# Three mixtures of experts of a decoder: blocks of tokens sorted by expert in all three, fetched by indirect reads

## The chip, the cores and the metric

The kernel runs on one core of a Trainium2 chip. One launch computes a whole decoder of four layers. The metric is the device time of that launch in microseconds (us). Three timed runs of the kernel before took 1896.66, 1902.3 and 1903.81 us; their median, 1902.3 us, is the time before. A further execution was recorded by the hardware profiler, and every figure of a view below comes from that one.

The engines of the core are named as in the profile: PE (matmuls) with its weight loads PEld, DVE and ACT (elementwise work, reductions, activations), POOL (elementwise work and the issue of indirect DMAs) and SP (which issues the plain DMAs here). Each takes its instructions in order; semaphores order them among each other.

## The reference

The input x has 4 x 256 = 1024 tokens of 128 numbers. Every layer adds a self attention, a cross attention and a feed-forward part to x, each on a normalised copy. Layer 0, 1 and 2 have a mixture of experts as feed-forward part; layer 3 has a plain one. Only the mixtures matter here (x stands for the normalised tokens):

```python
# layer 0: 32 experts, one for each token, inner width 256, and a shared expert
ids = argmax(x @ gate_w); s = sigmoid(max(x @ gate_w))
routed = (silu((x*s) @ g[ids]) * ((x*s) @ u[ids])) @ d[ids]
out = shared_swiglu(x) + routed
# layer 1: 8 experts, the best two for each token, inner width 512
w = softmax(top2(x @ gate_w.T))
out = sum_k w[k] * (silu(x @ w1[e_k].T) * (x @ w3[e_k].T)) @ w2[e_k].T
# layer 2: 8 experts, the best two for each token, inner width 512, with biases
p = softmax(x @ gate_w.T)
out = sum_k p[e_k] * (relu(x @ w1[e_k] + b1[e_k]) @ w2[e_k] + b2[e_k])
```

A mixture may be computed densely (each expert on all tokens, with weight nought for most) or sparsely (each expert only on its own tokens).

## The kernel before

x stays in SBUF for the whole launch as eight tiles of 128 tokens. The launch is a row of stages, each with its own pools of SBUF and PSUM: `layer_0` (both attentions), `ffn0`, `layer_1`, `strided_attention`, `ffn1`, `linear_attention`, `latent_attention`, `ffn2`, `layer_3`, `quantised_ffn`. The last lines of `decoder` call them in this order. The scheduler of the language puts the instructions of each engine in an order of its own and adds the semaphores; where a pool takes over the memory of one that is closed, its first users wait for the users of the old one.

**`ffn0` (line 895) is sparse.** `all_normalised_T` (793) gives the normalised tokens and their transposes, `logits_of` (799) the gate's logits, `top` (810) one-hot choices. `blocks_of` (830) sorts: it counts each expert's tokens (851), ranks each token within its expert (842 to 848) with triangular and all-one matrices, gives each expert as many blocks of 128 slots as it needs, and ends with `index` (a slot for each token) and `at` (for each block the columns of its expert in the weights). There are 1024/128 + 31 = 39 blocks at most, 4992 slots. A DRAM tensor `sent` is filled with zeros (908); then eight indirect DMAs on POOL store the tokens into their slots (920). Groups of four blocks are read back by plain DMAs (960) and transposed (966). For each block, `hidden` (970) multiplies by the gate and up matrices of its expert, whose columns the PE finds with a register loaded from `at` (890); SiLU and product follow; `turned` (982) transposes, `result` (989) multiplies by the down matrix, and each group is stored to `done` in DRAM (1003). The three work on blocks b, b-1 and b-2 in one turn. At the end eight indirect DMAs read each token's row from `done` (1020), and DVE adds it (1024). The shared expert (926 to 951) is computed between the stores and the blocks. The weights e0h (8 MB) and e0d (4 MB) lie in SBUF.

**`ffn1` (1043) and `ffn2` (1080) are dense.** Expert by expert, its weights come in one slab (1062, 1116). All 1024 tokens are multiplied (1069, 1120), put through the activation (1076 and 1077; 1127 and 1129), multiplied by the second matrix, and added to x with the weight of this expert for each token (`add_weighted`, 1026, with the matmuls of 1033 and the additions of 1039). In `ffn2` the second bias is one product of the weights with b2 (1107) and the first comes with the activation.

Between `ffn0` and `layer_1` SP loads the weights of all later attentions into the pool `late` (1692), 2 MB of them for `latent_attention` (w2x).

A matmul in f32 leaves two records in the trace.

Of the kernel before, what the change touches and what calls it, by code (L numbers as in the profile page):

```python
# [83 lines left out]
def _constants():  # L84
# [11 lines left out]
    iota = np.tile(np.arange(32), (P, 1))  # L96
# [11 lines left out]
) = np.cumsum([0, 128, 128, 72, 4, 32, 4, 4, 4, 1, 128, 64]).tolist()  # L108


def _layout(i):
# [53 lines left out]
    a["gates"] = _cat(  # L165
        f["L0_ffn_gate_w"], f["L1_ffn_gate_w"].T, f["L2_ffn_gate_w"].T,
        f["L2_ffn_b1"].reshape(8, 4, P).transpose(2, 0, 1).reshape(P, 32),
    )
    a["b2"] = f["L2_ffn_b2"]
# [8 lines left out]
    def down(w):  # L178
        return w.reshape(8, 4, P, P).transpose(0, 2, 1, 3).reshape(8, P, 512)

    a["e1"] = np.ascontiguousarray(np.concatenate([
        f["L1_ffn_w1"].transpose(0, 2, 1), f["L1_ffn_w3"].transpose(0, 2, 1),
        down(f["L1_ffn_w2"].transpose(0, 2, 1)),
    ], 2))
    a["e2"] = np.ascontiguousarray(np.concatenate([f["L2_ffn_w1"], down(f["L2_ffn_w2"])], 2))
# [7 lines left out]
def decoder(ctx: ExitStack, tc: tile.TileContext, dr, out):  # L193
# [636 lines left out]
    def blocks_of(pool, hots, size, widths):  # L830
# [7 lines left out]
        for i, h in enumerate(hots):  # L838
            V.tensor_copy(hb[:, i * NT : (i + 1) * NT, :], h)

# [8 lines left out]
        count = ps("t")[:n_e, :P]  # L849
        for i in range(n):  # L850
            T.matmul(count, lhsT=hb[:, i, :], rhs=onesb, start=i == 0, stop=i == n - 1)
# [12 lines left out]
        full = small.tile([P, 32], F32, tag="full", name="full")[:, :n_e]  # L864
        V.tensor_scalar(full, cum[:, 32 : 32 + n_e], partition, None, ALU.is_le)

        ex = small.tile([P, 3], F32, tag="ex", name="ex")
        V.tensor_reduce(ex[:, 2:3], full, AX.X, ALU.add)
        for i, wd in enumerate(widths):
            V.tensor_scalar(ex[:, i : i + 1], ex[:, 2:3], n_e - 1.0, float(wd), ALU.min, ALU.mult)  # L870
        xp = ps("t")
        for i in range(2):
            T.transpose(xp[:1, i * P : (i + 1) * P], ex[:, i : i + 1], ident)
        at = pool.tile([1, 2, P], I32, tag="at", name="at", bufs=1)
        V.tensor_copy(at, xp[:1, :S].rearrange("p (i b) -> p i b", i=2))
# [10 lines left out]
        return index, at  # L886

    def offset(at, i, b, most):

        return nc.values_load(  # L890
            at[0:1, i, b : b + 1], engines=[mybir.EngineType.PE], min_val=0, max_val=most,
            skip_runtime_bounds_check_because="the number of an expert, limited to the last one's",
        )

    def ffn0(wh):


        size = 39
        with ExitStack() as st:
            st.enter_context(psum_pool("psf0"))  # L900
            pool = st.enter_context(tc.tile_pool(name="ffn0", bufs=2))
            dram = st.enter_context(tc.tile_pool(name="ffn0d", bufs=1, space=bass.MemoryType.DRAM))
            wd = load("e0d", pool=pool)
            sent = dram.tile([size * P, D], F32, tag="sent", name="sent")
            done = dram.tile([size * P, D], F32, tag="done", name="done")
            nought = pool.tile([P, D], F32, tag="nought", name="nought", bufs=1)
            G.memset(nought, 0.0)
            nc.sync.dma_start(
                sent.rearrange("(n p) d -> p n d", p=P),
                nought.unsqueeze(1).to_broadcast([P, size, D]),  # L910
            )
            xn = [pool.tile([P, D], F32, tag=f"xn{t}", name=f"xn{t}", bufs=1) for t in range(NT)]
            xnT = all_normalised_T(pool, keep=xn, tag="t")
# [3 lines left out]
            index, at = blocks_of(pool, [hot], size, (512, 256))  # L917
            for t in range(NT):
                V.tensor_scalar(xn[t], xn[t], score[:, t : t + 1], None, ALU.mult)
                G.indirect_dma_start(  # L920
                    out=sent[:, :], out_offset=bass.IndirectOffsetOnAxis(ap=index[:, t : t + 1], axis=0),
                    in_=xn[t], in_offset=None,
                )


            for c in range(2):
# [24 lines left out]
                )  # L951


            groups = [range(b, min(b + 4, size)) for b in range(0, size, 4)]
            xbT, h, hT, y = {}, {}, {}, {}

            def fetch(g):
                n = len(groups[g])
                xb = pool.tile([P, 4, D], F32, tag="xb", name="xb", bufs=3)
                nc.sync.dma_start(  # L960
                    xb[:, :n, :],
                    sent[4 * g * P : (4 * g + n) * P, :].rearrange("(n p) d -> p n d", p=P),
                )
                tp = ps("t")
                for i in range(n):
                    T.transpose(tp[:, i * P : (i + 1) * P], xb[:, i, :], ident)
                xbT[g] = pool.tile([P, 512], F32, tag="xbT", name="xbT")
                A.copy(xbT[g][:, : n * P], tp[:, : n * P])

            def hidden(b):  # L970
                o = ps("g")
                at_h = offset(at, 0, b, 31 * 512)
                T.matmul(
                    o, lhsT=xbT[b // 4][:, b % 4 * P : (b % 4 + 1) * P],
                    rhs=wh[:, bass.ds(at_h, 512)], start=True, stop=True,
                )
                sg = pool.tile([P, 256], F32, tag="sg", name="sg", bufs=3)
                A.activation(sg, o[:, :256], AF.Silu)
                h[b] = pool.tile([P, 256], F32, tag="h", name="h", bufs=3)
                V.tensor_tensor(h[b], sg, o[:, 256:], ALU.mult)  # L980

            def turned(b):
                tp = ps("t")
                for i in range(2):
                    T.transpose(tp[:, i * P : (i + 1) * P], h[b][:, i * P : (i + 1) * P], ident)
                hT[b] = pool.tile([P, 256], F32, tag="hT", name="hT", bufs=3)
                V.tensor_copy(hT[b], tp[:, :256])

            def result(b):
                g, i = b // 4, b % 4  # L990
                if i == 0:
                    y[g] = ps("y")
                at_d = offset(at, 1, b, 31 * 256)
                for ic in range(2):
                    T.matmul(
                        y[g][:, i * P : (i + 1) * P], lhsT=hT[b][:, ic * P : (ic + 1) * P],
                        rhs=wd[:, bass.ds(at_d + ic * P, P)], start=ic == 0, stop=ic == 1,
                    )
                if b == groups[g][-1]:
                    n = len(groups[g])  # L1000
                    ys = pool.tile([P, 4, D], F32, tag="ys", name="ys")
                    A.copy(ys[:, :n, :], y[g][:, : n * P].rearrange("p (n d) -> p n d", n=n))
# [6 lines left out]
            for b in range(size + 2):  # L1009
                if b % 4 == 1 and b // 4 + 1 < len(groups):  # L1010
                    fetch(b // 4 + 1)
                if b < size:
                    hidden(b)
# [707 lines left out]
```

## Time and profile before

| | us |
|---|---|
| median of three timed runs | 1902.3 |
| profiled execution | 1916.55 |
| its span, first to last instruction | 1914.7 |
| ffn0: last addition of layer 0's attention to the first matmul of layer 1 | 321.0 to 463.1 |
| ffn1: last addition of the strided attention to the first matmul of the linear attention | 619.3 to 799.4 |
| ffn2: last addition of the latent attention to the first matmul of layer 3 | 1406.3 to 1537.1 |

How to read the views. The page gives busy time, share of the span and count of instructions of each engine, and then groups: line, engine, operation, what is written and read, shapes, count, busy time in us, mean time of one in ns, and after the second bar the idle time of the engine just before, with what ended most of it. The timeline gives start, duration, engine, line, operation and count of runs of equal instructions, and in brackets the idle time before. The list of DMA issues gives tile, queue, count, KB of each and median us from issue to landing. PEq, PEldq, SPq and so on are an engine's sequencer. The profiled execution is 14 us longer than the median of the others; differences within it are read as shares of it.

### The profile page before, as it was taken

To read this page: it belongs to the slowest core of one execution; us is meant where nothing else is said; L and a number is where in the kernel's file an instruction comes from. 1 tells how busy PE (TensorE), PEld (TensorE's weight loads), DVE (VectorE), ACT (ScalarE), POOL (GpSimd) and SP (SyncE) were. 2 spreads that over 40 slices of the span, in tenths; PEclk is the share of its full clock that TensorE was granted. 3 is DMA by queue.
4 is the path that set the end of the run, shared out by engine and by line. 5 is a ranking of instruction groups with operands and counts; after the bars stand their busy time and mean duration, and the time that the engine had idled before them with its cause. 6 is when DMAs were issued, how large, how long until landed. Compare 5 with 4: busy or idle time off the path is not lost. (4 is left out here: it accounts for less than half of the span.)

```text
span 1914.7 us, 27552 instructions
## 1 busy us (share of the span) xinstructions
PE 1651.3 (86%) x10756; PEld 887.9 (46%) x10756; DVE 884.3 (46%) x2886; ACT 709.2 (37%) x1307; POOL 239.1 (12%) x391
## 2 busy tenths in 40 slices
PE   6999997694977999755889999999999989999873
PEld 3443333362456566544344554545567744433332
DVE  4565552242744333544743434434233355655526
ACT  1444445131621212100466566566621114344441
POOL 5221000105120000221200000000000041211000
PEclk9999997796966899855989999999999959999985
DMA  7000002323000110000000000000011000000000
GB/s 262 1 1 1 1 1 101 90 60 105 2 1 14 53 49 17 1 0 6 1 1 1 1 1 1 1 1 1 1 45 34 12 26 1 1 1 1 1 1 11
DMA packets 26193, 43.69 MB, mean 23 GB/s; under 512 B 2504, under 2 KB 20176, under 8 KB 24784
## 3 DMA queue, kind: packets, MB, share of 16 engines
q1 hardware_dynamic: 25552, 40.89, 6.1%
q8 instruction: 85, 1.39, 0.3%
q0 software_dynamic: 512, 1.05, 0.2%
q14 instruction: 44, 0.36, 0.1%
HBM read 35.77 MB, written 6.16 MB: 22 GB/s over the span
## 5 line engine op out<-in xcount | busy, mean ns | idle before, releaser
L492 PE MATMUL s<-kc,qm 32*128 32x256 f32 (+1 forms) x1024 | 239.0, 579 | 10.4 <-POOL qm L449 4.2
L554 PE MATMUL s<-qm,kc 32*128 32x512 f32 (+1 forms) x896 | 230.5, 629 | 1.4 <-POOL qm L449 1.4
L571 ACT ACTIVATE pr<-s 128x512 f32<-128x512 f32 x256 | 137.9, 596 | 187.8 <-PE s L554 184.9
L499 DVE TENSOR_REDUCE mx<-s 128x1 f32<-128x512 f32 (+1 forms) x192 | 123.2, 686 | 110.4 <-PE s L554 98.9
L1431 ACT ACTIVATE ss<-ss,ntop 128x768 f32<-128x768 f32 x128 | 118.6, 928 | 100.6 <-DVE ntop L1429 100.3
L285 POOL TENSOR_SCALAR ve<-mv 128x2 f32<-128x2 f32 (+1 forms) x64 | 14.2, 223 | 1124.9 <-DVE mv L283 1120.4
L590 PE MATMUL o<-pr,v 128*32 128x256 f32 (+1 forms) x1792 | 146.6, 395 | 4.1 <-ACT os L596 3.7
L492 PEld LDWEIGHTS s<-kc,qm 32*128 32x128 f32 x1024 | 98.1, 211 | 76.9 <-DVE mx L503 26.2
L1033 PEld LDWEIGHTS pt<-slab,hT 128*128 128x128 f32 x1024 | 118.5, 192 | 11.3 <-issue 8.8
L1425 DVE CUSTOM_DVE_ANT_0 ss<-f,n 128x512 f32<-128x512 f32 x128 | 83.7, 688 | 80.3 <-PE f L1420 80.3
L1033 PE MATMUL pt<-slab,hT 128*128 128x128 f32 x1024 | 119.3, 276 | 0.0
L503 DVE CUSTOM_DVE_ANT_0 junk<-s,nmif 128x512 bf16<-128x512 f32 x128 | 83.3, 689 | 70.8 <-PE s L492 70.7
L1069 PE MATMUL sc<-xnT,slab 128*128 128x512 f32 x256 | 115.4, 605 | 0.0
L1491 PE MATMUL o<-pr,v 128*64 128x256 f32 x768 | 113.6, 402 | 0.0
L573 ACT ACTIVATE pr<-s,n 128x512 f32<-128x512 f32 x128 | 80.3, 685 | 73.9 <-PE s L554 73.6
L1471 PE MATMUL s<-qT,kT 64*128 64x256 f32 x768 | 107.5, 394 | 0.0
L449 POOL TENSOR_SCALAR qm<-q,consts 128x256 f32<-128x256 f32 x80 | 73.1, 930 | 207.3 <-ACT q L446 147.8
L590 PEld LDWEIGHTS o<-pr,v 128*32 128x32 f32 x1792 | 40.3, 110 | 122.3 <-issue 99.6
L1478 ACT ACTIVATE pr<-s,n 128x512 f32<-128x512 f32 x128 | 80.6, 679 | 27.8 <-PE s L1471 27.6
L548 PE MATMUL s<-mT,selg 12*128 12x256 bf16 x768 | 78.5, 282 | 7.8 <-ACT pr L573 5.7
L1420 PE MATMUL f<-kT,qT 64*128 64x512 f32 x256 | 78.6, 628 | 2.4 <-ACT kT L274 1.2
L1076 ACT ACTIVATE sg<-sc 128x1024 f32<-128x1024 f32 x32 | 32.8, 1024 | 125.9 <-DVE x L1039 66.9
(374 smaller groups left out, 2631.9 us busy)
## 6 DMA issues: line engine op xcount, KB each, us to landing
e0h<-in_e0h SPq DMA_DIRECT2D x8, 1024.0 KB, 13.6
slab<-in_e SPq DMA_DIRECT2D x8, 768.0 KB, 4.3
e0d<-in_e0d SPq DMA_DIRECT2D x1, 4096.0 KB, 12.9
slab<-in_e SPq DMA_DIRECT2D x8, 512.0 KB, 3.4
sent<-nought SPq DMA_DIRECT2D x1, 2496.0 KB
xb<-sent SPq DMA_DIRECT2D x9, 256.0 KB, 2.9
done<-ys SPq DMA_DIRECT2D x9, 256.0 KB, 2.2
w2x<-in_w2x SPq DMA_DIRECT2D x1, 2050.0 KB, 9.3
```

Source lines behind the costliest of these rows:

```text
L492: T.matmul(sc[:, i, :], lhsT=u.qm[r, g + i, qt * P : (qt + 1) * P], rhs=u.kc[r, :], start=u.row_mask is None, stop=True,)
L499: V.tensor_reduce(u.mx[:, qt, j, g : g + per], sc, AX.X, ALU.max)
L503: V.tensor_tensor_reduce(junk[:, : u.nk], sc[:, i, :], u.rows_mask(qt), 1.0, -3e38, ALU.add, ALU.max, accum_out=u.mx[:, qt, j, g + i : g + ...
L554: T.matmul(sc, lhsT=u.kc[r, kt * P : (kt + 1) * P], rhs=u.qm[r, gp : gp + 2, first:], start=u.clip, stop=True,)
L571: A.activation(dst, sc, AF.Exp)
L590: T.matmul(u.po[gp][32 * j : 32 * j + 32, i, first:], lhsT=u.v[:, kt, 4 * j + gp + i, :], rhs=u.pr[gp, kt, j][:, i, first:], start=kt + i ...
L1033: T.matmul(y[:, i * P : (i + 1) * P], lhsT=hT[:, ic, t * P : (t + 1) * P], rhs=wd[:, ic * P : (ic + 1) * P], start=ic == 0, stop=ic == 3,)
L1069: T.matmul(o[:, k * 512 : (k + 1) * 512], lhsT=slab[:, m * 512 + ic * P : m * 512 + (ic + 1) * P], rhs=xnT[:, k * 512 : (k + 1) * 512], st ...
L1425: V.tensor_tensor_reduce(ss[qt][h][:, :SK], sc[h], neg1[:, b * SK : (b + 1) * SK], 1.0, -3e38, ALU.add, ALU.max, accum_out=mx[:, qt, h, 1:2],)
L1431: A.activation(ss[qt][h], ss[qt][h], AF.Exp, bias=ntop[:, qt, h, c : c + 1], accum_out=total[:, qt, h, c : c + 1],)
L1471: T.matmul(sc[h][:, i, :], lhsT=kT[u, c][hrow[h], kt * P : (kt + 1) * P], rhs=qT[u, c][hrow[h], :], start=False, stop=i == 1,)
L1491: T.matmul(po[u, g][hrow[h], i, :], lhsT=v[u][:, kt, n * hd : (n + 1) * hd], rhs=pr[u, g, kt, h][:, i, :], start=kt + i == 0, stop=kt + i ...
```

## The change

All three mixtures now go through one function, `mixture`, which is the sparse way of `ffn0` with another way into the blocks. The normalised tokens are stored to `sent` in their own order by one plain DMA. `blocks_of` computes besides `index` its inverse, `token`: for each slot the number of its token. Each token's slot is split into place (low seven bits) and block; place is made a one-hot matrix, block a one-hot matrix times the tile's number and times the partition; their product, summed over the tiles, has the two parts of the number, and slots that nobody holds get 0. POOL then fetches each block by one indirect read of `sent`, four to a group; two groups are fetched ahead, and the third during the first turn. Nothing is stored indirectly and nothing is zeroed. Blocks of layers 1 and 2 are 16 + 7 = 23; each token has two slots, and at the end two rows are read back for each tile, 16 indirect reads, each added with its weight. The biases of layer 2 come in as matmuls of an all-one matrix with three bf16 parts of each bias.

The weights of layers 1 and 2 are laid side by side and loaded whole: e1h (4 MB) and e1d (2 MB) into the memory of e0h before `layer_1`, e2h and e2d (2 MB each) in `ffn2` itself; w2x moves from `late` to a pool of its own, opened after `ffn1`. In layer 0 the scaling by the score moves from DVE to POOL, and in `blocks_of` the counts come before the ranks.

The core of the diff:

```diff
@@ blocks_of
+        count = ps("t")[:n_e, :P]
+        for i in range(n):
+            T.matmul(count, lhsT=hb[:, i, :], rhs=onesb, start=i == 0, stop=i == n - 1)
         rank = ps("g")[:, : n * n_e]
...
+        V.tensor_scalar(split[:, 0, :], index, 7, None, ALU.logical_shift_right)
+        V.tensor_scalar(split[:, 1, :], index, P - 1, None, ALU.bitwise_and)
+        V.tensor_copy(where, split)
+        V.tensor_tensor(
+            place, iota.unsqueeze(1).to_broadcast([P, n, P]),
+            where[:, 1, :].unsqueeze(2).to_broadcast([P, n, P]), ALU.is_equal,
+        )
+        V.tensor_tensor(
+            block[:, 1], iota[:, :size].unsqueeze(1).to_broadcast([P, n, size]),
+            where[:, 0, :].unsqueeze(2).to_broadcast([P, n, size]), ALU.is_equal,
+        )
+        for i in range(len(hots)):
+            half = slice(i * NT, (i + 1) * NT)
+            V.tensor_tensor(
+                block[:, 0, half], block[:, 1, half],
+                iota[:, :NT].unsqueeze(2).to_broadcast([P, NT, size]), ALU.mult,
+            )
+        V.tensor_scalar(block[:, 1], block[:, 1], partition, None, ALU.mult)
+        for t in range(n):
+            T.matmul(who, lhsT=place[:, t, :], rhs=block[:, :, t, :], start=t == 0, stop=t == n - 1)
+        V.tensor_copy(low, who[:, 1, :])
+        V.scalar_tensor_tensor(token, who[:, 0, :], float(P), low, ALU.mult, ALU.add)
...
@@ mixture
+        nc.sync.dma_start(sent.rearrange("(t p) d -> p t d", p=P), rows_)
+        index, token, at = blocks_of(pool, hots, size, (n1, n2) if biases is None else (n1, n2, P))
+        def fetch(g):
+            xb = pool.tile([P, 4, D], F32, tag="xb", name="xb", bufs=3)
+            for i, b in enumerate(groups[g]):
+                G.indirect_dma_start(
+                    out=xb[:, i, :], out_offset=None, in_=sent[:, :],
+                    in_offset=bass.IndirectOffsetOnAxis(ap=token[:, b : b + 1], axis=0),
+                )
+            return xb
+        def hidden(b):
+            o = [ps("g") for _ in range(0, n1, 512)]
+            at_h = offset(0, b, (n_e - 1) * n1)
+            for i, p in enumerate(o):
+                if biases is not None:
+                    T.matmul(p, lhsT=onesb[0:3, :], rhs=biases[0:3, bass.ds(at_h, 512)], ...)
+                T.matmul(p, lhsT=xbT[b // 4][...], rhs=wh[:, bass.ds(at_h + 512 * i, 512)], ...)
...
+        fetched = {g: fetch(g) for g in range(2)}
+        rows_T(0, fetched[0])
+        for b in range(size + 2):
+            g = b // 4 + 1
+            if b % 4 == 0 and g + 1 < len(groups):
+                fetched[g + 1] = fetch(g + 1)
+            if b % 4 == 1 and g < len(groups):
+                rows_T(g, fetched[g])
+            if b < size:
+                hidden(b)
+            if 1 <= b <= size:
+                turned(b - 1)
+            if b >= 2:
+                result(b - 2)
+        for t in range(NT):
+            for i in range(k):
+                back = pool.tile([P, D], F32, tag="back", name="back", bufs=6)
+                n = i * NT + t
+                G.indirect_dma_start(
+                    out=back, out_offset=None, in_=done[:, :],
+                    in_offset=bass.IndirectOffsetOnAxis(ap=index[:, n : n + 1], axis=0),
+                )
...
+                    V.scalar_tensor_tensor(
+                        x[t], back, weights[i][:, t : t + 1], x[t], ALU.mult, ALU.add
+                    )
@@ decoder, the calls
-    w1x, w2a, w2x, b2, w3a, w3x, w3f = (
-        load(k, pool=late) for k in ("w1x", "w2a", "w2x", "b2", "w3a", "w3x", "w3f")
-    )
-    layer_1()
-    other(strided_attention, ffn1, linear_attention)
-    latent_attention()
-    other(ffn2)
+    with tc.tile_pool(name="e1", bufs=1) as experts:
+        e1h, e1d = load("e1h", pool=experts), load("e1d", pool=experts)
+        w1x, w2a, w3a, w3x, w3f = (
+            load(k, pool=late) for k in ("w1x", "w2a", "w3a", "w3x", "w3f")
+        )
+        layer_1()
+        other(strided_attention)
+        ffn1(e1h, e1d)
+    with tc.tile_pool(name="w2x", bufs=1) as experts:
+        w2x = load("w2x", pool=experts)
+        other(linear_attention)
+        latent_attention()
+    ffn2()
```

`rows_T` transposes a fetched group, `turned` and `result` are as before with the widths of the layer; lines of the changed kernel from L843 on lie elsewhere than before.

## The prediction

> **What bounds the kernel now.** I read the page first, then busy time by stretches of the span, then the timeline at the edges of the three mixtures, then the DMA issues. The page says that TensorE carries the kernel, and names the two matmul groups of the dense mixtures, L1033 (both, second product) and L1069 (layer 1, first product).
>
> ```profile
> PE 1651.3 (86%) x10756; PEld 887.9 (46%) x10756; DVE 884.3 (46%) x2886; ACT 709.2 (37%) x1307; POOL 239.1 (12%) x391
> ...
> L1033 PE MATMUL pt<-slab,hT 128*128 128x128 f32 x1024 | 119.3, 276 | 0.0
> L1069 PE MATMUL sc<-xnT,slab 128*128 128x512 f32 x256 | 115.4, 605 | 0.0
> ```
>
> An f32 matmul leaves two records, which overlap: L1033 costs 119.3/1024 = 0.117 us a record, L1069 115.4/256 = 0.45. The stretches are the middles of the stages (columns: PE, weight loads, DVE, ACT, POOL busy; granted clock; DMA share; GB/s):
>
> ```profile
> 342.50:367.40 24.90, 8.51 (x48) 6.16 (x46) 3.10 (x5) 1.92 (x4) 7.97 (x8) 0.71 0.17 53
> 372.00:437.00 65.00, 64.52 (x331) 42.24 (x329) 28.44 (x76) 23.72 (x54) 0.00 (x0) 1.00 0.20 58
> 437.00:463.10 26.10, 0.87 (x7) 0.56 (x6) 6.11 (x26) 0.48 (x1) 13.97 (x22) 0.59 0.49 179
> ...
> 627.00:799.40 172.40, 170.54 (x769) 106.61 (x769) 62.23 (x142) 34.47 (x35) 2.13 (x9) 0.98 0.07 23
> ...
> 1412.00:1531.50 119.50, 117.64 (x667) 84.48 (x666) 45.57 (x132) 19.25 (x20) 1.84 (x4) 0.99 0.07 23
> ```
>
> Rows four and five are layers 1 and 2: PE is busy all along, so what PE does there is their time. Rows one to three are layer 0, already in blocks: 25 us of scatters, 65 us of blocks on PE, and 26 us in which rows come back and PE does nothing. The timeline shows the price of indirect DMAs there:
>
> ```profile
> 342.56 1.24 POOL L920 DMA_INDIRECT sent<-xn,index  x1 [17.01 <-DVE index L885]
> ...
> 345.34 0.97 POOL L920 DMA_INDIRECT sent<-xn,index  x1 [1.53 <-DMA sent<-xn,index]
> 347.87 0.96 POOL L920 DMA_INDIRECT sent<-xn,index  x1 [1.56 <-DMA sent<-xn,index]
> ...
> 446.79 0.98 POOL L1020 DMA_INDIRECT back<-done,index  x1 [85.49 <-DMA w3x<-in_w3x]
> 448.08 0.96 POOL L1020 DMA_INDIRECT back<-done,index  x1 [0.30 <-issue]
> ...
> 459.35 0.29 DVE L1024 TENSOR_TENSOR x<-x,back 128x128 f32<-128x128 f32 x1 [1.42 <-DMA back<-done,index]
> ...
> 459.77 0.95 POOL L430 MEMSET v<- 128x1024 f32 x1
> ```
>
> A scatter waits for the one before it: 2.5 us each. Gathers only queue on POOL: 1.25 us each. The memset of layer 1's first pool comes when the last row is added: a stage's first pool waits for the whole pool before it. DMA prices and the register load that a dynamic matmul needs:
>
> ```profile
> e0d<-in_e0d SPq DMA_DIRECT2D x1, 4096.0 KB, 12.9
> ...
> done<-ys SPq DMA_DIRECT2D x9, 256.0 KB, 2.2
> ...
> done<-ys SPq DMA_DIRECT2D x1, 192.0 KB, 7.6
> back<-done,index POOLq DMA_INDIRECT x8, 2.6
> ```
>
> ```profile
> L890 PEldq TENSOR_LOAD <-at x78: 294/299/495, 366.4 to 436.7; - x78
> ```
>
> **What the Trainium skill says.** "DMA: Bandwidth & Descriptors", Queues, rings and completion order: each DMA engine takes a queue's descriptors in ring order. The trace agrees: the last done store, behind w1x, w2a and w2x, lands after 7.6 us, the others after 2.2. The same page, Issuing engines are not separate DMA queues: gathers and loads share the 16 DMA engines; here they landed in 2.6 us beside the last weights. "TensorE: Matmul & The Clock Gate", What's actually happening: the array runs at half clock until it has been busy some 3.4 us. In the trace it took about 6: a 512-column record goes at 0.43 us warm, 0.86 at 367.4 after a pause.
>
> **Layer 0 (before: 321.0 to 463.1, first matmul of the next stage).** Zero fill and scatters go. The counts now precede the ranks on PE and the scaling has left DVE, so index comes about 1.6 us earlier, at 340.5. Added before the first gather: split and where 0.6; place, 1024 elements, 1.2 (as L1077, 1.22); three block operations at 0.42 (as L823); the shared expert's DVE work that the compiled order puts between them, 3 x 0.69; eight products 1.0 (L851: 8 in 1.03); two evictions and hops 0.9. The tile token, which the gathers read, is there at 347.5. The scaling on POOL (8 x 0.79, as L289 there) ends at 339 and the plain store lands before 343: hidden. The order of PE puts the transposes of block group 1 ahead of the second block, so 8 gathers must land: 347.9 + 8 x 1.25 + 1.7 = 359.6. Counted at the fourth block, where both are warm, 364.5 against 372.2: 7.7 earlier. After that POOL needs 1.25 a block and PE 1.77 (69.1 us for 39), so fetching is hidden. At the end SP issues e1h (4 MB) as soon as the last block has read e0h, at 427.4 (before: w1x at 435.1), and the last done store stands behind it: 12.9 + 0.6 + hops, 441.6 instead of 446.0. Eight gathers follow; with 4 MB more weights beside them I add 0 to 3 us. **-5** (bounds -10, +3). The w3f sums stand early in DVE's order; w3f lands about 453.6 (8.2 MB at the 356 GB/s of 435.1 to 448.5), 5 us before DVE gets there.
>
> **Layer 1 (619.3 to 799.4).** The e1 loads are long over. Removed: 171 us of PE. Routing up to the one-hot ends at 629.8 as now. Then: casts 0.5; 32 products for counts and ranks 4.1; counts' chain, cum and base 0.7 beyond them; to index 1.6; split, where 0.5; place, 2048 elements, 2.3; block operations 1.4; 16 products 2.1; token 0.5: 643.3. Eight gathers: 643.5 + 10 + 1.7 = 655.2, second block at 655.9. Price of a block on PE: 4 records x 0.43, 4 transposes and 8 records of the second product x 0.107, a row transpose 0.107: 3.1, with layer 0's gap of 0.13 **3.25** (DVE 1.4, ACT 0.9, POOL 1.25 beside it). Last first product ends 655.9 + 0.3 + 21 x 3.25 + 1.7 = 726.2. Two steps of the pipeline remain, 4.0, eviction and issue 0.9. w2x (2 MB) is issued at 726.4 before the last done store, which lands at 734.8 rather than 733.5. Then 16 gathers at 1.25, the last landing after 2.65, adds 0.35: 756.8, next stage's PE at 757.4. **-42** (-50, -32).
>
> **Layer 2 (1406.3 to 1537.1).** Its weights are loaded at its start, 4 MB, landed at 1419.5 (12.9), then sent, 1421.5; the three bias parts go POOL, DRAM and back by about 1427.5. All lie beside the routing: without dense matmuls in between, one-hot at 1416.8, token 13.1 later, 1429.9, eight gathers to 1441.8. A block: 2 x 0.43 + bf16 bias rows 0.21 and 0.05 (L548: 78.5/768 = 0.10 for 256 bf16 columns) + 12 x 0.107 + 0.107 = 2.5; two kinds more of register work (loads of 0.3 us, mostly under matmuls): **2.7**. 1442.1 + 0.5 + 21 x 2.7 + 1.07 = 1500.4; drain and store 7.3; 16 gathers and add 22: last add at 1529.7, against 1531.5. **-2** (-12, +10): the dense stage was short, so routing (35 us) and return (25 us), with PE idle, eat what 23 blocks for 64 save.
>
> The compiled order of the other stages is that of before on PE, so nothing else moves. Sum -49. The profiled execution took 1916.6 (span 1914.7), 0.75% over the median of the three timed runs, so -49 x 0.9926: 1902.3 - 48.6 = **1854**.
>
> **Unknown.** Most slots of layer 0 are empty and all read row 0. No gather of before does; reading one 2 KB row into 128 partitions (mrow, 256 KB) landed in 3.1 us, done's 256 KB in 2.2, so I take nothing, at most 0.4 a gather, which still fits under 1.77. One-hot operations: nearest rows, +-3 a stage.
>
> **Rivals.** (A) Gathers go one by one at the scatters' 2.5 us. For: L920; POOL also shares its ports. Against: L1020's 1.25, and in the compiled order a fetch waits for the one eight before. It would cost layer 0 +19 in the loop (10 against 7.1 a group) and +10 on return, layers 1 and 2 each +10 at the front and +20 on return: +89, 1942, slower than before; slope 71 us per us, so it decides from 1.93 us a gather on. 5%. (B) Dynamic addresses starve PE: two or three loads and up to seven register operations a block. For: 0.13 gaps in layer 0. Against: 0.3 a load, and no growth there with three dynamic matmuls. At 0.7 a block, 46 blocks: +32, 1886. 6%. (C) Next stages start on x[0], x[1] and don't wait for the last gather: 12 of 16 gathers hidden twice, -13 each: 1828. Against: the memset at 459.77. 4%. My forecast as worked out: 85%.
>
> **Range.** The stages' bounds together give about +-14 around 1854: 1840 to 1868; the order's unknowns and part of B widen it to 1836 to 1882. What a measurement can tell from no change is about 0.5%, 9.5 us. Faster 0.92 (forecast, B, C), same 0.03 (mild forms of A and B), slower 0.05 (A).
>
> **What would show it.** First dynamic matmul near 356, 652 and 1438 less what went before; gathers 1.25 us apart; blocks 1.77, 3.25 and 2.7; last done stores late by the load ahead; 20 us of PE silence before the stage after layer 1. Wrong if gathers stand at 2 us or more, or if blocks of layers 1 and 2 take over 3.9 and 3.4.

## The result, and the profile after

The changed kernel takes 1894.43 us (median of 9 runs, 1891.96 to 1901.43), the kernel before 1903.19 (9 runs, 1896.66 to 1914.46): a ratio of 0.9955, with a 95% interval of 0.9933 to 0.9977. That is 8.8 us less, where 48 were forecast; the time lies above the range of 1836 to 1882. The profiled execution of the changed kernel took 1891.96 us (span 1890.2), that of the kernel before 1916.55: between these two it is 24.6 us. A run more than 1.5% above the fastest of its kernel counts as slow and is left out of the comparisons; there is one, a run of actdone below (1888.6 us).

First the page of the changed kernel: busy time, and the row of the new gathers.

```profile
PE 1522.2 (81%) x10216; PEld 803.5 (43%) x10217; DVE 868.3 (46%) x2862; ACT 692.6 (37%) x1317; POOL 348.2 (18%) x512
...
L946 POOL DMA_INDIRECT xb<-sent,token x85 | 80.9, 952 | 91.9 <-PE t L956 35.3
```

PE lost 129 us of work, and the 85 gathers cost 0.95 us each, as L1020's did before. Both are as forecast, so the loss is in waiting. The same stretches as before the change (columns: PE, weight loads, DVE, ACT, POOL busy; granted clock; DMA share; GB/s). Rows 1 to 4 are layer 0's first blocks, its other blocks, the wait for the last store, and the return; then blocks and return of layer 1, and blocks and return of layer 2:

```profile
349.60:372.00 22.40, 13.59 (x38) 7.51 (x39) 3.56 (x9) 2.59 (x7) 11.52 (x13) 0.65 0.30 40
372.00:432.00 60.00, 59.91 (x299) 38.40 (x297) 25.27 (x68) 22.73 (x51) 17.94 (x19) 1.00 0.35 58
432.00:445.50 13.50, 1.75 (x10) 1.24 (x10) 0.70 (x2) 0.48 (x1) 0.00 (x0) 0.69 1.03 397
445.50:461.60 16.10, 0.00 (x0) 0.00 (x0) 4.81 (x24) 0.00 (x0) 13.67 (x21) 0.50 0.60 236
649.00:732.00 83.00, 76.07 (x371) 49.91 (x372) 29.21 (x45) 19.96 (x34) 15.41 (x17) 0.92 0.12 30
732.00:760.00 28.00, 2.20 (x19) 1.93 (x17) 6.57 (x22) 0.48 (x1) 12.41 (x14) 0.60 0.34 111
1405.00:1480.00 75.00, 71.83 (x383) 46.77 (x382) 22.57 (x34) 12.96 (x23) 12.79 (x14) 0.92 0.14 31
1480.00:1506.00 26.00, 0.00 (x0) 0.00 (x0) 8.91 (x33) 0.33 (x1) 18.05 (x23) 0.53 0.17 48
```

Once layer 0's blocks run (row 2), PE is full at full clock. In the first 22 us (row 1) it is busy for 13.6, at a clock of 0.65. The timeline shows what happens there. A bracket gives the idle time before the instruction and what ended it; "remote" means that a semaphore rose just before it, but that the trace holds no instruction or DMA to which that rise belongs.

```profile
339.80 1.21 POOL L946 DMA_INDIRECT xb<-sent,token  x1 [9.27 <-DVE token L904]
...
356.49 1.02 PE L969 MATMUL g<-e0h,xbT 128*128 x2
...
361.17 0.42 DVE L981 COPY hT<-t 128x256 f32<-128x256 f32 x1 [4.30 <-remote]
...
361.65 0.82 PE L990 MATMUL y<-e0d,hT 128*128 x4 [3.91 <-issue]
...
363.83 0.94 POOL L946 DMA_INDIRECT xb<-sent,token  x1 [0.30 <-issue]
368.20 0.66 ACT L1054 ACTIVATE sg<-g 128x256 f32<-128x256 f32 x2 [11.79 <-remote]
...
369.19 0.66 PE L979 MATMUL t<-consts,h 128*128 128x128 f32 x2 [4.77 <-DVE h L1055]
...
372.05 0.94 POOL L946 DMA_INDIRECT xb<-sent,token  x1 [7.27 <-PE t L956]
```

From 339.80 to 364.8 POOL issues 20 gathers without a break, 1.25 us apart: three buffers for groups of four, and two of them free again as soon as their rows are transposed. The first product of the fourth block starts on PE at 356.49 and lasts 1 us; ACT, which needs nothing else, reads it at 368.20. DVE waits in the same way for a transpose. PE then stops for 3.9 and 4.8 us and goes on at half clock. All is over 3.4 us after the last gather of the row of 20. I call this a pause. (Where nothing pauses, the row of gathers isn't 20 long in layer 0 but 32, as on chip B below: PE frees the buffers in time.) The view of waits has the like in all three mixtures (columns: us in total, times, longest):

```profile
ACT sg L1054 <- remote: 11.8, 1, 11.8
DVE hT L981 <- remote: 11.0, 2, 6.7
DVE h L1055 <- remote: 7.9, 1, 7.9
...
DVE h L1156 <- remote: 3.7, 1, 3.7
```

The kernel before has no wait of this kind. The end of layer 0 came as forecast: the last store stands behind the 4 MB of e1h, and the first gather that waits for it starts 10.7 us after its issue.

```profile
431.32 0.46 SPq L218 DMA_DIRECT2D e1h<-in_e1h  x1
...
434.83 0.36 SPq L1006 DMA_DIRECT2D done<-ys  x1
...
445.51 0.94 POOL L1030 DMA_INDIRECT back<-done,index  x1 [41.20 <-DMA done<-ys]
```

The length of each mixture, from its first normalised row to its last addition, in us:

| | layer 0 | layer 1 | layer 2 | sum |
|---|---|---|---|---|
| before | 138.3 | 179.2 | 125.0 | 442.5 |
| forecast (by its steps of -5, -42, -2) | 133.3 | 137.2 | 123.0 | 393.5 |
| after | 142.9 | 147.2 | 134.1 | 424.2 |

Each is about 10 us over its forecast.

### The profile page after: what moved, and what is told of

Its sections match the earlier page's. It is cut to its first block, busy times and chain, and to the rows that moved or that the text cites. A ratio compares the mean times of both kernels' runs of the same rounds, so it can differ in the third digit from the quotient of the medians.

```text
span 1890.2 us, 27097 instructions
## 1 busy us (share of the span) xinstructions
PE 1522.2 (81%) x10216; PEld 803.5 (43%) x10217; DVE 868.3 (46%) x2862; ACT 692.6 (37%) x1317; POOL 348.2 (18%) x512
## 4 chain that ended last, share of the span: by engine, by line
PE 67%; DVE 12%; ACT 6%; issue 5%; POOL 5%; DMA 3%; another core or an unknown queue 1%; POOLq 0%; DVEq 0%; ACTq 0%; SPq 0%
PE s L493 7%; PE s L555 7%; PE g L969 5%; PE o L1523 5%; PE o L591 4%; PE s L1503 4%; PE f L1452 3%; PE y L990 3%; PE f L1410 2%; PE s L549 2%; PE f L1438 2%; ACT pr L574 2%; PE t L979 2%; DVE junk L504 2%; PE s L542 2%
## 5 line engine op out<-in xcount | busy, mean ns | idle before, releaser
L574 ACT ACTIVATE pr<-s,n 128x512 f32<-128x512 f32 x128 | 80.4, 685 | 71.3 <-PE s L555 71.0
L946 POOL DMA_INDIRECT xb<-sent,token x85 | 80.9, 952 | 91.9 <-PE t L956 35.3
L981 DVE COPY hT<-t 128x512 f32<-128x512 f32 (+1 forms) x85 | 48.1, 566 | 77.5 <-PE t L979 50.3
L1523 PEld LDWEIGHTS o<-pr,v 128*64 128x64 f32 x768 | 48.9, 138 | 62.4 <-issue 32.1
L555 PEld LDWEIGHTS s<-qm,kc 32*128 32x128 f32 x896 | 69.9, 198 | 9.5 <-issue 5.2
```

What stands on the lines that cost most here:

```text
L555: T.matmul(sc, lhsT=u.kc[r, kt * P : (kt + 1) * P], rhs=u.qm[r, gp : gp + 2, first:], start=u.clip, stop=True,)
L574: A.activation(dst, sc, AF.Exp, bias=u.key_bias(kt))
L1523: T.matmul(po[u, g][hrow[h], i, :], lhsT=v[u][:, kt, n * hd : (n + 1) * hd], rhs=pr[u, g, kt, h][:, i, :], start=kt + i == 0, stop=kt + i ...
```

## The experiments

They ran on five chips, A to E; the time of a kernel is compared only with others on its own chip. The time of the kernel before is that of the same chip. Which chip the first measurement ran on isn't on record. Theories for the pause: H, the hot row (all empty slots of the blocks read row 0 of sent); T, the train (20 gathers in a row, whatever they read). Q, a separate theory: the return starts late since the last store of a mixture stands behind the next load.

| chip | kernel | us, median (range) | before | ratio, 95% |
|---|---|---|---|---|
| A | spread | 1861.2 (1858.2 to 1865.8) | 1902.1 | 0.9782, 0.9737 to 0.9827 |
| A | gated | 1863.8 (1859.5 to 1875.5) | 1902.1 | 0.9814, 0.9762 to 0.9867 |
| A | actdone | 1871.4 (1859.7 to 1872.6) | 1902.1 | 0.9803, 0.9739 to 0.9867 |
| A | all3 | 1874.2 (1869.2 to 1882.4) | 1902.1 | 0.9851, 0.9798 to 0.9904 |
| B | after_again | 1868.2 (1863.8 to 1877.8) | 1906.8 | 0.9793, 0.9740 to 0.9846 |
| B | after_shift | 1869.3 (1859.0 to 1873.3) | 1906.8 | 0.9789, 0.9728 to 0.9850 |
| B | lateload | 1860.8 (1855.9 to 1865.6) | 1906.8 | 0.9771, 0.9717 to 0.9824 |
| B | spread_late | 1855.8 (1853.7 to 1859.4) | 1906.8 | 0.9737, 0.9685 to 0.9790 |
| C | after_third | 1896.6 (1891.0 to 1902.4) | 1899.4 | 0.9984, 0.9966 to 1.0002 |
| C | gated_again | 1869.4 (1868.5 to 1879.9) | 1899.4 | 0.9865, 0.9835 to 0.9894 |
| C | spread_again | 1894.3 (1889.0 to 1902.9) | 1899.4 | 0.9975, 0.9960 to 0.9989 |
| C | late2 | 1888.6 (1877.9 to 1889.9) | 1899.4 | 0.9951, 0.9934 to 0.9967 |
| D | after_fourth | 1869.5 (1862.5 to 1876.5) | 1899.6 | 0.9835, 0.9773 to 0.9897 |
| D | train16 | 1868.1 (1866.0 to 1870.2) | 1899.6 | 0.9827, 0.9781 to 0.9874 |
| D | gated_late | 1851.5 (1846.3 to 1867.5) | 1899.6 | 0.9760, 0.9698 to 0.9822 |
| D | gated_late_dense2 | 1844.0 (1842.8 to 1847.4) | 1899.6 | 0.9704, 0.9668 to 0.9740 |
| E | after_fifth | 1901.8 (1894.0 to 1907.0) | 1904.0 | 0.9974, 0.9937 to 1.0010 |
| E | train16_again | 1881.8 (1876.0 to 1887.7) | 1904.0 | 0.9881, 0.9808 to 0.9955 |

### Chip A: three cures, and a surprise

Distinct rows for the empty slots (spread). A third set of columns in the one-hot product says which slots are filled:

```diff
...
-        V.tensor_copy(low, who[:, 1, :])
+        V.tensor_scalar(low, who[:, 2, :], partition, None, ALU.mult)
+        V.scalar_tensor_tensor(low, who[:, 1, :], partition, low, ALU.add, ALU.subtract)
```

> Edit: an empty slot of a block no longer reads row 0 of sent; lane p reads row p instead (a third set of columns in the one-hot product tells which slots are filled). Theory H (hot row): the pauses of 8.7, 6.6 and 2.9 us of PE in the first blocks of the three mixtures, and the cold clock after them, come from 128 lanes reading one row; they go, and the time falls by 20 to 27 us, to about 1870; the 4 KB packets of the gathers of layer 0, which took 500 to 700 ns on average after the first eight gathers, fall to the 220 ns of layers 1 and 2. Theory T (train): the pauses come with the unbroken train of 20 gathers that POOL issues at the start of a mixture, whatever they read: packets get shorter, the pauses stay, the time is within 5 us of 1894.

A shorter train (gated). The fetch of a later group first writes into its buffer from the block before, so POOL has to wait for it:

```diff
+            if after_block is not None:
+                G.tensor_copy(xb[:, :, 0], h[after_block][:, 0:4])
...
-                fetched[g + 1] = fetch(g + 1)
+                fetched[g + 1] = fetch(g + 1, b - 1 if b else None)
```

> Edit: from the fourth group of blocks on, POOL first copies four columns of the hidden block before (a 128x4 copy into the buffer that is to be filled), so that the train of 20 gathers at the start of a mixture is cut to 12, and each later group of four waits for its turn. Rows read are the same. Theory T (train): the pauses of 8.7, 6.6 and 2.9 us go, and with them the cold clock: 18 to 27 us less, 1867 to 1876. Theory H (hot row): the pauses of layer 0 stay, where most slots are empty; time within 6 us of 1894, if anything slower.

The last store of each mixture from another queue (actdone):

```diff
-                nc.sync.dma_start(
+                queue = nc.scalar if b == size - 1 else nc.sync
+                queue.dma_start(
```

> Edit: only the last done store of each mixture is issued by ACT, on its own queue, instead of by SP behind the next load (e1h in layer 0, w2x in layer 1). Theory Q (order in the queue): the store lands some 3 us after its issue instead of 10.6 and 8.9 us, and the return begins 7 and 6 us earlier: 13 us less, about 1881. Rival B (the DMA engines are full of the load's bytes either way): the return begins at most 2 us earlier in each, time 1890 to 1895.

And the three together:

> All three edits together: spread rows for empty slots, trains cut to 12, last done store from ACT. If T, H and Q each hold for a part, the time is 1894 less 22 (pauses) less 13 (last store): about 1859. If only Q holds, about 1881; if only the pauses go, about 1872.

None of the four has a pause: the view of waits shows no "remote" in any, and PE stands for at most 1.3 us in the blocks of a mixture. But actdone has the trains and the hot row as they were, so on this chip neither H nor T could be told: the pause may not come with the kernel alone. (The unaltered kernel wasn't run on this chip.) actdone also spoke against Q as I had put it. In layer 0 the first gather that waits for the store on ACT's own queue starts 16.9 us after the store's issue, not some 3, and not 10.7 as behind e1h:

```profile
424.35 0.46 SPq L218 DMA_DIRECT2D e1h<-in_e1h  x1
...
427.46 0.43 SPq L218 DMA_DIRECT2D w3f<-in_w3f  x1
427.92 0.38 ACTq L1007 DMA_DIRECT2D done<-ys  x1
444.87 0.94 POOL L1031 DMA_INDIRECT back<-done,index  x1 [47.49 <-DMA w3a<-in_w3a]
```

The reader is to see that every load up to w3f is issued before the store. The view puts POOL's release down to the load of w3a, but the trace has that load's last completion at 445.1, after the gather has started, and the store's own at 444.0: it is the store that POOL waits for. The Trainium skill, "DMA: Bandwidth & Descriptors", Queues, rings and completion order, says that each DMA engine takes turns between queues, packet by packet. The trace agrees: the store's 384 packets of 512 bytes start one by one between 431.6 and 443.6, among packets of up to 32 KB of the 8 MB of loads. Behind e1h in one queue the store waits for 4 MB alone. In layer 1, where only w2x is ahead, the first gather starts 9.0 us after the store's issue, as in the unaltered kernel. all3 contains this edit, which explains 8 of the 13 us by which it is slower than spread; its layer 0 takes 139.3 us to the last addition, that of spread 131.5.

### Chip B: the changed kernel once more, and the loads behind the return

The unaltered kernel again (after_again):

> The changed kernel once more, unaltered, beside the others of this call. In the earlier runs the pauses of PE in the first blocks were gone in a kernel whose only edit is the issuer of the last done store (which comes 60 us later). Theory P (the pauses belong to one loading or one chip, not to the kernel): here they are gone too, the time is 1860 to 1875. Theory L (the pauses hang on how this very program lies in memory, and so come with every loading of it): they are there again at 43, 44 and 44 us into the three mixtures, time 1891 to 1897. Theories H and T of the earlier runs (hot row, train) also expect them again.

With one memset that nothing reads, so that everything lies elsewhere (after_shift):

```diff
+    unused = const.tile([P, 4], F32, tag="unused", name="unused")
+    G.memset(unused, 0.0)
```

> The changed kernel with one memset of a 128x4 tile that nothing reads, added to POOL at the start of the program, so that its instructions and tiles lie elsewhere; nothing else differs. Theory L: pauses gone or moved, 1860 to 1875, while the unaltered kernel has them. Theory P: same time as the unaltered kernel beside it. Theories H and T: pauses as before, 1891 to 1897.

The loads held back (lateload), and the same on top of distinct rows (spread_late):

```diff
         t = (pool or const).tile(shape, dtype, tag=name, name=name, bufs=1)
+        if behind is not None:
+            V.tensor_copy(t[0:1, 0:1], behind[0:1, 0:1])
         nc.sync.dma_start(t, src)
...
-        e1h, e1d = load("e1h", pool=experts), load("e1d", pool=experts)
+        e1h, e1d = (load(k, pool=experts, behind=x[1]) for k in ("e1h", "e1d"))
```

> Edit: every load that follows a mixture (w1x to w3f, e1h, e1d after layer 0; w2x after layer 1) first has one element written from x[0] or x[1] by DVE, so that it is issued when the first rows have come back, behind the last done store instead of ahead of it. Theory Q: that store lands 3 us after its issue instead of 10.6 and 9; the return begins 7 and 6 us earlier, 13 us less than the unaltered kernel beside it (with pauses 1881, without about 1855). Rival: the loads now lie beside the gathers of the return and slow these by as much; the last addition of layer 0 comes at most 3 us earlier.

> Spread rows for empty slots together with the loads behind the return. If the pauses don't come (as in the run with spread rows) and Q holds: 1861 less 13, about 1848. If the loads only move the wait: about 1861.

The unaltered kernel takes 1868.2 us here, without pauses; the shifted one is level with it. So the pause depends on the chip or on the loading of the program (P). Holding the loads back showed what holds of Q and what of its rival. In layer 0 the first gather starts 3.0 us after the store's issue, but the gathers then run beside the loads:

```profile
432.20 0.35 SPq L220 DMA_DIRECT2D w1x<-in_w1x  x1
...
434.77 0.38 SPq L220 DMA_DIRECT2D e1h<-in_e1h  x1
...
437.74 0.95 POOL L1032 DMA_INDIRECT back<-done,index  x1 [0.30 <-issue]
...
443.67 0.29 DVE L1037 TENSOR_TENSOR x<-x,back 128x128 f32<-128x128 f32 x1 [1.90 <-DMA back<-done,index]
```

The last gather is issued at 437.74; additions still come 2.6 us apart at 443.67, and the last ends 134.2 us into the stage, against 132.1 in the unaltered kernel: all lost again, as the rival said. In layer 1 the last addition came 5.6 us earlier (132.2 against 137.8). By the medians lateload is 7.4 us faster than the unaltered kernel, where Q said 13, and the ranges of the two overlap; spread_late, at 1855.8, lies between its two expectations.

The gathers' prices in DMA time show the hot row. After_again, then spread on chip A, in the first 22 us of layer 0's blocks:

```profile
349.60:372.00 22.40, 20.39 (x84) 12.14 (x84) 6.62 (x18) 6.76 (x15) 16.91 (x19) 0.79 0.47 62
```

```profile
349.60:372.00 22.40, 21.39 (x90) 12.80 (x91) 7.93 (x21) 7.14 (x16) 16.91 (x19) 0.85 0.24 71
```

With one row for all empty slots the DMA engines are busy for 47% at 62 GB/s, with distinct rows for 24% at 71. Per byte it is 2.2 times as dear. These stretches have stores in them and come from two chips; on chip C, the first 20 gathers alone (1.31 MB, from 340 to 372 us) keep the DMA engines busy for 26.9% in the unaltered kernel and for 13.8% with distinct rows, 1.9 times as long. POOL issues a gather each 1.25 us either way, and without pauses PE's blocks of layer 0 take 69.4 (after_again) and 69.0 us (spread): a hot row was there, and cost next to nothing.

### Chip C: a chip that pauses

The unaltered kernel (after_third), short trains (gated_again) and distinct rows (spread_again):

> The changed kernel, unaltered, a third time. It took 1894 in its first measurement, with pauses of PE in all three mixtures, and 1868 without them in the second. Theory P (the pauses belong to a chip or a loading of the program): one of the two is found again, 1891 to 1897 with pauses at 43 to 44 us into each mixture, or 1860 to 1878 without any; nothing between. Rival R (they come at random from execution to execution): times spread between both inside one set of rounds.

> The trains of 20 gathers cut to 12, beside the unaltered kernel of the same call. If the unaltered kernel pauses here: T (train) says no pause and 20 us less, H (hot row) says pauses as in the unaltered one. If it does not pause, both are level within 0.5%, since nothing else hangs on the gathers' issue.

> Distinct rows for empty slots, beside the unaltered kernel of the same call. If the unaltered kernel pauses here: H says no pause and 20 us less, T says pauses as in the unaltered one. If it does not pause: level within 0.5%, as the long packets of the hot row stay under POOL's 1.25 us a gather.

Here the unaltered kernel pauses in all three mixtures, in each of its 8 runs by the times (1891.0 to 1902.4; R, that pauses come at random, falls). The kernel with distinct rows pauses as well; its view of waits:

```profile
ACT sg L1055 <- remote: 20.2, 3, 9.3
DVE hT L982 <- remote: 13.5, 2, 9.4
ACT h L1155 <- remote: 10.0, 1, 10.0
```

The gated kernel, on the same chip, has not one such wait and is 27 us faster than the unaltered one. Its POOL stops where it should, in layer 0 for 4.0 us after the twelfth gather, and PE goes on. Below its first 22 us, and those of the unaltered kernel on this chip:

```profile
354.72 0.94 POOL L948 DMA_INDIRECT xb<-sent,token  x1 [0.30 <-issue]
359.68 0.19 POOL L946 COPY xb<-h 128x4 f32<-128x4 f32 x1 [4.02 <-DVE h L1057]
360.40 0.97 POOL L948 DMA_INDIRECT xb<-sent,token  x1 [0.53 <-POOL xb L946]
```

```profile
349.60:372.00 22.40, 21.36 (x91) 13.01 (x92) 7.77 (x21) 7.14 (x16) 12.54 (x15) 0.85 0.27 50
```

```profile
349.60:372.00 22.40, 11.32 (x30) 5.53 (x31) 2.77 (x7) 3.09 (x7) 13.86 (x15) 0.73 0.33 48
```

PE is busy for 21.4 of these 22.4 us, against 11.3 in the unaltered kernel. H falls as the cause of the pauses, T stands. The mixtures take 134.2, 137.4 and 128.2 us in the gated kernel and 143.5, 147.9 and 133.7 in the unaltered one beside it: 25.3 us of the 27. The layout of the program (L) has little left: kernels with different instructions pause at the same place of the same three stages, while the gated one does not.

The traces hold one thing more that sets these chips apart. Within 3 us of a gather's start PE, DVE and ACT end instructions that raise a semaphore. In the first measurement and on chips C and E many of these rises have no record: 81 of 225 in the first profile, 74 of 224 in after_third, and also 127 of 343 in the gated kernel, which doesn't pause. On chips A, B and D at most one is missing. So "remote" says when an engine started, and not when its signal rose. And since every run on record has a recorded span and clock, none shows whether a pause would come without the recording.

On this chip I also ran the loads behind the whole return, on top of spread (late2: lateload's edit with x[7] in place of x[0] and x[1], and w3f first):

> Spread rows, and the loads after layers 0 and 1 held until the last row of the mixture has been added (one element of each written from x[7]), w3f first. Theory Q with contention: the run with loads behind x[0] and x[1] gained 7 us at the last done store of layer 0 and lost all of it again, as its last gather landed 11 us after its issue beside 8 MB of loads; with the loads behind x[7] gathers land in 2 us, layer 0's last addition comes near 123 us into the stage instead of 131, layer 1's near 132 instead of 138: 14 us less than the spread kernel beside it, 1846 to 1850 where that takes 1861. Rival: layer 1's attention now waits for w3f or w1x, and gives back 3 us or more.

```profile
437.46 0.94 POOL L1033 DMA_INDIRECT back<-done,index  x1 [33.61 <-DMA done<-ys]
...
446.45 0.98 POOL L1033 DMA_INDIRECT back<-done,index  x1 [0.30 <-issue]
...
448.90 0.30 DVE L1038 TENSOR_TENSOR x<-x,back 128x128 f32<-128x128 f32 x1 [0.59 <-DMA back<-done,index]
449.50 0.34 SPq L220 DMA_DIRECT2D w3f<-in_w3f  x1
```

In this timeline of layer 0's return the last gather now lands in time for an addition 2.5 us after its issue, and the loads begin after that. Beside spread_again the last additions come 134.9 us into layer 0 instead of 142.7, and 141.8 into layer 1 instead of 147.9. The mixtures give what Q expected, 13.9 us, though both kernels pause. The spans of the two profiled executions differ by 11.2 (1876.0 and 1887.2); by the medians it is 5.7 only, and late2's profiled execution is the fastest of its five (the others took 1887.9 to 1889.9). That the later stages wait for the held loads isn't seen in them (from layer 0's last addition to layer 1's mixture 161.1 us against 160.4), so the rest is not explained.

### Chips D and E: the length of the train, and the sum

First the unaltered kernel and train16 on chip D, then both on chip E:

> The changed kernel, unaltered, as the control of this call: 1890 to 1902 with pauses 18 to 25 us after the first gather of each mixture, or 1859 to 1878 without any, according to the chip.

> Only the fetches from the fifth group of blocks on wait for a hidden block, so that the first train is 16 gathers instead of 20 (12 in the gated kernel). In the traces the pauses began 18 to 22 us after the first gather, when 14 to 18 had been issued. On a chip that pauses: if the pause needs the train to run past 16, none is left, 1866 to 1876; if 14 are enough, pauses stay, 1885 to 1897. On a chip without pauses: level with the control within 0.5%.

> The changed kernel, unaltered, as the control of this call: 1890 to 1902 with pauses, or 1859 to 1878 without any, according to the chip.

> The first train 16 gathers instead of 20. If the control pauses: no pause and 1866 to 1876 if the train must run past 16; pauses and 1885 to 1897 if 14 are enough. If the control doesn't pause: level with it, and the length stays open.

The edit, against that of gated:

```diff
-                fetched[g + 1] = fetch(g + 1, b - 1 if b else None)
+                fetched[g + 1] = fetch(g + 1, b - 1 if b > 4 else None)
```

Chip D doesn't pause, so train16 told nothing there. Chip E does. The unaltered kernel's PE stands for 9.2, 6.6 and 6.0 us in the blocks of the three mixtures, train16's for 5.3, 2.3 and 1.6; on chip C the kernel with trains of 12 had 1.3, 0 and 0. So 16 are enough for a pause, and PE's standing grows with the train. By the length of the mixtures it is less plain: train16 takes 142.6, 143.2 and 130.5 us, the unaltered kernel 143.1, 147.7 and 137.3, so layer 0 gained next to nothing. Neither expectation had it in between; the waits of train16 on chip E:

```profile
ACT sg L1056 <- remote: 6.7, 2, 5.6
DVE h L1057 <- remote: 5.0, 1, 5.0
DVE hT L983 <- remote: 3.9, 1, 3.9
```

Then both causes away together (trains of 12, loads behind x[7]), and with layer 2 dense again:

> Trains cut to 12, and the loads after layers 0 and 1 held until the last row has been added (w3f first). Theory T plus Q: last additions near 126, 132 and 128 us into the three mixtures (gated alone 134, 137, 128), so 13 us less than the gated kernel: 1852 to 1858 on any chip, with no pauses. Rival: half of it is given back in the stages that wait for the held loads, 1860 to 1865.

> As gated_late, with layer 2's mixture dense as in the kernel before (its weights in slabs, all tokens through all experts). By the stages' lengths dense takes 125.2 us from the start to the last addition and blocks 128.3: 3 us less than gated_late, 1849 to 1855. If the sparse stage is worth what I forecast (2 us less than dense) it is 2 us more.

```diff
-    ffn2()
+    other(ffn2)
```

(with ffn2, add_weighted and the weights' layout of the kernel before.) gated_late takes 1851.5 us; its mixtures take 125.0, 131.8 and 129.9 us, against the expected 126, 132 and 128. Leaving layer 2 dense takes 7.5 us off that, where 3 were expected; in the traces layer 2 takes 125.0 us instead of 129.9, which is 4.9 of it. One of gated_late's four times, 1867.5, lies far from the others, and the intervals of the two ratios overlap: that dense is the faster one is likely by these runs, and its size isn't shown. The page of gated_late_dense2:

```profile
PE 1549.5 (84%) x10437; PEld 829.0 (45%) x10438; DVE 872.8 (47%) x2885; ACT 696.3 (38%) x1310; POOL 311.2 (17%) x478
```

It beats both kernels: 1844.0 us, 0.9704 of the kernel before (0.9668 to 0.9740), 25.5 us less than the changed kernel on the same chip. It was not run on a chip that pauses.

## Why the prediction was wrong

**Bounds and removed work.** Right. PE's time in the dense mixtures of layers 1 and 2 was the time of these stages, and 129 us of it went.

**The way to the first gather.** Right within 2.5 us: forecast 26.5, 24.0 and 23.6 us from the start of a stage to the token tile, measured 24.9, 21.5 and 21.9 (first profile) from its first normalised row, which comes 0.2 us later.

**The price of a gather.** Right: 0.95 us, 1.25 apart, without exception. Rival A is out. The hot row was named as unknown and taken as nothing; its packets are dear, and it did cost nothing that the times can tell.

**The blocks hide the fetching.** This is the step that failed: "After that POOL needs 1.25 a block and PE 1.77 (69.1 us for 39), so fetching is hidden." I compared rates, and took POOL's head start for a benefit. The head start is a train of 20 gathers, and in the first measurement and on chips C and E, ACT, DVE and PE start late towards its end, ACT once 10.7 us after its input was done. Layers 0, 1 and 2 lose 11, 10 and 6 to 9 us by it, and trains of 12 bring it back on chip C (25.3 us in the three mixtures), but for some 2 us in layer 0, whose blocks then take 71.3 us. No rival had this: A asked what a gather takes, B what a block takes, neither what the queue of gathers does to the others. Without pauses the blocks were as forecast: 69.2 to 69.4 us from the first product of layer 0's first block to that of the last one (38 steps of 1.77 are 67.3, and the first run at half clock), and 71.0 for layer 1's 22 steps, 3.23 each, where 3.25 were forecast.

**The last store behind the next load.** Right in layer 0: forecast to land 120.6 us into the stage, and without pauses the first gather that waits for it started at 120.3 and 119.7. In layer 1 w2x was issued when the last second product had been read, not after the last first product as I had put it; the blocks' being 2 us shorter hid the error. I had booked this wait and not asked whether it was worth avoiding: it was, 14 us in two stages by the traces of late2 and spread_again on chip C, though 5.7 by the medians, as long as the loads then keep off the gathers. On chip D, where short trains alone bring nothing (train16), gated_late is 18 us faster than the unaltered kernel.

**The return.** Right: 16 gathers and the last addition 21.5 us in layer 1, 22 forecast.

**The sum.** On a chip without pauses the mixtures take 132.1, 137.8 and 128.3 us (after_again), 44.3 less than before; 49 were forecast. The term that was mis-sized is layer 2's block, 2.9 us (63.9 for 22 steps) instead of 2.7: the stage became 3.3 us longer, where I had it 2 shorter. The -5 of layer 0 doesn't come out of its own figures: a store 4.4 us earlier, less 0 to 3 for the weights, gives -4.4 to -1.4; without pauses the stage became 6.2 us shorter. With pauses it is 18.3 less, and that is what the first measurement shows.

**From the profile to the median.** Times fell by 6 to 15 us less than the mixtures did: 38.6 and 30.1 on chips B and D against 44 and 45; with pauses 8.8, 2.8 and 2.2 against 18, 17 and 14. My factor of 0.9926 allowed for 0.4. The profiled execution of before was 13.4 us over its median, and a part of that may lie in the stages that I took the difference from; with one profile of that kernel it can't be placed.

So the gain in the mixtures was forecast rightly to 5 us where nothing pauses, and the change brings 39 and 30 us on chips B and D; what was missed is a stall of which the profile of before had no example, since its indirect DMAs came at most 8 in a row and with PE idle beside them.

What stays open: what holds the engines back, why two of five chips have it (each chip was used on one occasion only), and whether the recording has a part in it. The trace shows that instructions with all their inputs done start late, that the waits begin 16.6 us or more after the train's first gather, when some 14 gathers or more have been issued (the last of 12 starts after 14.0), and that in every trace with pauses, trains of 16 too, the last late start comes at most 5.3 us after the start of the train's last gather. It doesn't show the holder.

## What to carry to other kernels

An engine that runs ahead is not free: ask how long its longest unbroken queue of indirect DMAs is, and cap it at what the consumer needs next (here 12 gathers). Keep the next stage's loads away from the last store and the gathers of this one, in time and not by another queue: in layer 0, beside the gathers they cost as much as they did ahead of the store. And since a change can move one chip by 2% and another by nothing, run the unaltered kernel again beside every experiment before believing a cure: on chip A three different edits looked like a cure.

## What the runs showed of the hardware

- In a train of 20 indirect gathers on POOL (1.25 us apart) ACT and DVE started late, ACT by 10.7 us in the first profile. With 16 PE stood for 5.3, 2.3 and 1.6 us instead of 9.2, 6.6 and 6.0 (chip E); with 12 no such wait was seen (chip C). Two of five chips and the first measurement showed it; on three chips trains of 20 and more passed without. Where it was seen, a quarter and more of the semaphore rises near gathers have no record, with 12 too.
- Gathers of which most lanes read one row of 512 bytes kept the DMA engines busy 1.9 times as long as gathers of distinct rows (26.9% and 13.8% of the same 32 us on chip C, 1.31 MB each).
- After a 192 KB store on ACT's own queue, issued after 8 MB of loads on SP's, the first gather that waits for it started 16.9 us later; in SP's queue behind the first 4 MB it was 10.7, ahead of them 3.0.
